# Output biases of two expert mixtures: one bf16 product over 96 rows in place of a small f32 product, on one Trainium2 core

## The chip, the core and the metric

The kernel runs on one core of one Trainium2 chip. A core has a matrix engine (TensorE, here PE), three engines for element-wise work (VectorE or DVE, ScalarE or ACT, GpSimd or POOL), and SyncE (SP), whose queue issues all of this kernel's DMAs. Operands lie in SBUF, matmuls accumulate in PSUM. The metric is the device time of one execution in microseconds (us).

## The reference, cut to what matters

Eight stages work on 625 nodes of 768 features, a graph layer and a mixture of experts in each of four layers. Each stage normalizes its input and adds its result to x. Two of the mixtures have an output bias, and the change is about these:

```python
# layer 1 (cut): 8 experts, two for each node
gates_full = jnp.zeros((T, E)).at[jnp.arange(T)[:, None], top_idx].add(gates)
def body(acc, p):
    w1, bb1, w2, bb2, g = p
    h = jax.nn.gelu(xn2 @ w1 + bb1, approximate=False)
    return (acc + g[:, None] * (h @ w2 + bb2), None)

# layer 2 (cut): 4 experts with 1024 slots each
h = jax.nn.gelu(jnp.einsum('besd,edh->besh', slots, w1) + b1[None, :, None, :])
y = jnp.einsum('besh,ehd->besd', h, w2) + b2[None, :, None, :]
out = jnp.einsum('besd,bnes->bnd', y, combine)
```

In layer 1 the bias' share of a node's output is its 8 gates times the matrix `b2` of 8 x 768. In layer 2 it is the sum of `combine` over each expert's slots (4 numbers for a node) times a matrix of 4 x 768. Layers 0 and 3 have mixtures of the same form as layer 1's, without a bias.

## The kernel before

The nodes are five tiles of 125 (`TILES`). Weights, products and activations are f32. Most large products are done by a scheme of seven half-size products with sums of blocks ahead (on DVE and POOL) and behind (on DVE).

The program is written for a framework that allots each engine its instructions in an order near the written one, and puts in the waits. The trace shows where it departs from the written order: for example the first matmul of product 5 runs ahead of product 7 in `half_rest`.

`experts` (from line 972) is the mixture of layers 0, 1 and 3. Its 1536 hidden columns are 12 chunks of 128, done in pairs. For a pair c, `first(c)` does products 1 and 2, `sums(c)` puts four block sums on POOL (L338 to L342), and `rest(c)` does products 6, 7, 5, 4, 3 (`half_rest`, L412 are its additions) and the gelu (L1010, ACT). A function handed to `half_rest` runs behind product 6. In `rest(0)` that is `choose`: the router's logits are turned (L260) and `gates` works out on DVE which two experts a node takes and with which weights (L935 to L961), then splits each gate into three bf16 parts in the tile `gb`, by five small operations (L964 to L968). In `rest(2)` it is `chosen`: five matmuls with the identity turn `gb` (L1034) and a copy puts it into `gT3`, 24 rows of 625 (L1038). In layer 1 five f32 transposes (L1042) and a copy (L1043) also put the f32 gates into `gT`, 8 rows. `gate(c)` spreads one expert's gate over its 128 hidden rows by a product with a matrix of ones and zeros (L129, 24 rows, bf16) and multiplies the chunk `hg` with it (L1018). `beside` runs some unrelated sums of products (L1309) on DVE, fed by DMAs.

`down` (from line 1059) is the second product, 12 chunks into 2 x 384 columns. Tile 0 is done directly, tiles 1 and 2 and tiles 3 and 4 in pairs, by seven products of six chunks (`prod`, recorded at L136, with additions at L1125). Where there is a bias, tile 0's two products and products 4, 2, 5 and 3 of each pair end with one more f32 matmul of 8 rows, `gT` or `db` times `b2t`. `db` is the difference of the gates of the pair's two tiles (POOL, L1103), since product 3 needs their difference. `b2t` is loaded by one DMA (L978).

`L2_ffn` (from line 1585) ends in a part that works tile by tile. `scale` multiplies the sums of three experts by factors (L1770), `weights` forms the last expert's exponentials (L1725 on DVE, L1728 on ACT), `last_sums` does the last expert's products, its copies, and the factors `fd` of 4 numbers a node (L1837 to L1845). `turn_sums` transposes the tile (L1798), and `fd` with it (L1804). ACT copies the first (L1802, L1805), DVE the second (L1806). `out` does six f32 matmuls (L1817) and one of 4 rows for the bias (L1822), for each half of the columns. The bias is loaded by one DMA (L1787). `final` normalizes the tile for the next stage; it adds the next bias on POOL (L225).

Of the kernel before, what the change touches and what calls it, by code (L numbers as in the profile page):

```python
# [17 lines left out]
N = 625  # L18
# [17 lines left out]
class Net:  # L36
# [362 lines left out]
    def half_rest(self, prods, U2, top, bottom, between=None):  # L399
# [16 lines left out]
        if between:  # L416
            between()
        prod(7, a2)
        add(C21, U2, a2)
        prod(5, b1)  # L420
# [505 lines left out]
    def gates(self, over_all):  # L926
# [35 lines left out]
        gb = sp.tile([P, NT, NEXP, 3], BF16, tag="gb", name="gb", bufs=1)  # L962
        r = sp.tile([P, NT, NEXP], F32, tag="gr", name="gr", bufs=1)
        nc.vector.tensor_copy(gb[:, :, :, 0], lg)  # L964
        nc.vector.tensor_tensor(r, lg, gb[:, :, :, 0], ALU.subtract)
        nc.vector.tensor_copy(gb[:, :, :, 1], r)
        nc.vector.tensor_tensor(r, r, gb[:, :, :, 1], ALU.subtract)
        nc.vector.tensor_copy(gb[:, :, :, 2], r)  # L968
        return gb

    def experts(self, over_all, w1, w2, gelu, b1=None, b2=None, after=None, beside=None):

        nc, tc, a, x = self.nc, self.tc, self.a, self.x
        with tc.tile_pool(name="moe", bufs=1) as big, ExitStack() as up_pool:
            bc = self.column(b1, NF) if b1 else None
            if b2:
                b2t = big.tile([NEXP, D], F32, name="b2t")
                nc.sync.dma_start(b2t, a[b2])  # L978
            hg = big.tile([128, NF, N], F32, name="hg")
            gT3 = big.tile([3 * NEXP, N], BF16, name="gT3")  # L980
            gT = big.tile([NEXP, N], F32, name="gT") if b2 else None
# [20 lines left out]
            def rest(c, between=None):  # L1002
# [11 lines left out]
            def gate(c):  # L1014
                gv = self.nv(self.ps(), 128)
                self.mm_nodes(gv, [sel[:, c * 128 : (c + 1) * 128]], [self.n3(gT3)])
                h = self.n3(hg[:, c, :])
                nc.vector.tensor_tensor(h, h, gv, ALU.mult)  # L1018
# [6 lines left out]
            turned, gb = self.logits(big), []  # L1025

            def choose():
                turned()
                gb.append(self.gates(over_all))

            def chosen():
                pv = self.nv(self.ps(), 3 * NEXP)
                for t in range(NT):
                    nc.tensor.matmul(  # L1034
                        pv[:, t, :], gb[0][:, t].rearrange("p e i -> p (e i)"),
# [3 lines left out]
                if b2:  # L1039
                    pv = self.nv(self.ps(), NEXP)  # L1040
                    for t in range(NT):
                        nc.tensor.transpose(pv[:, t, :], self.lg[:, t, :], self.ident[:P, :P])  # L1042
                    nc.vector.tensor_copy(self.n3(gT), pv)  # L1043

            rest(0, choose)
            for c in range(2, NF + 2, 2):
                if c < NF:
                    if c not in begun:
                        first(c)
                    rest(c, chosen if c == 2 else None)  # L1050
# [1263 lines left out]
```

## Time and profile before

| what | value |
|---|---|
| median of 3 runs | 1917.44 us (1917.02 to 1918.27) |
| the profiled execution | 1917.89 us |
| its span, first to last instruction | 1916.2 us |
| mean granted clock of TensorE | 0.988 |
| busy: PE, DVE, POOL, ACT | 1849.2, 1129.8, 601.8, 526.0 us |
| layer 1's mixture: up products / `down` | from about 717 / 797.2 to 879.7 us |
| layer 2's tile-by-tile part | about 1352 to 1424 us |
| layer 0's and layer 3's gates | about 246 to 257 / 1777 to 1788 us |

The page that the profile prints has the busy time of each engine, the chain of work that ended last, and the costliest groups of instructions. In a group's or timeline's line "L136 PE MATMUL ps<-b2t,gT 8*125 8x384 f32", the first number pair is the stationary operand's rows and columns, the second the moving operand's. In a timeline, the first two numbers are the start and the length in us; lines that belong together are merged, xN tells how many records; the bracket is the engine's idle time before it and what ended it. PEld is the loading of a matmul's stationary operand. A matmul's length includes its way through the array, so the time that one costs in a stream is read from start to start.

### The profile page before, as it was taken

To read this page: it belongs to the slowest core of one execution; us is meant where nothing else is said; L and a number is where in the kernel's file an instruction comes from. 1 tells how busy PE (TensorE), PEld (TensorE's weight loads), DVE (VectorE), ACT (ScalarE), POOL (GpSimd) and SP (SyncE) were. 2 spreads that over 40 slices of the span, in tenths; PEclk is the share of its full clock that TensorE was granted. 3 is DMA by queue.
4 is the path that set the end of the run, shared out by engine and by line. 5 is a ranking of instruction groups with operands and counts; after the bars stand their busy time and mean duration, and the time that the engine had idled before them with its cause. 6 is when DMAs were issued, how large, how long until landed. Compare 5 with 4: busy or idle time off the path is not lost.

```text
span 1916.2 us, 21703 instructions
## 1 busy us (share of the span) xinstructions
PE 1849.2 (97%) x8314; PEld 1273.0 (66%) x8314; DVE 1129.8 (59%) x2227; ACT 526.0 (27%) x960; POOL 601.8 (31%) x514
## 2 busy tenths in 40 slices
PE   7968899999999999999999999999999999999999
PEld 6844565555677766655555788878767888556655
DVE  8789866547566756663935464554545555145552
ACT  2379721002244532100110131331314233111200
POOL 1079634234410052433106322231025321402341
PEclk9969999999999999999999999999999999999999
DMA  2040111211300022213410211001011121020111
GB/s 69 21 143 34 40 53 50 77 58 34 95 13 25 1 99 94 67 53 131 142 66 34 74 64 36 25 25 34 1 44 37 44 66 64 1 99 25 50 33 32
DMA packets 64021, 103.16 MB, mean 54 GB/s; under 512 B 7301, under 2 KB 37223, under 8 KB 63918
## 3 DMA queue, kind: packets, MB, share of 16 engines
q1 hardware_dynamic: 63658, 101.69, 16.1%
q8 instruction: 66, 1.08, 0.2%
q14 instruction: 37, 0.30, 0.1%
q10 hardware_dynamic: 260, 0.09, 0.0%
HBM read 99.81 MB, written 1.95 MB: 53 GB/s over the span
## 4 chain that ended last, share of the span: by engine, by line
PE 86%; DVE 7%; POOL 3%; ACT 2%; issue 1%; DMA 1%; ACTq 0%; DVEq 0%; POOLq 0%; SPq 0%
PE ps L136 66%; PE ps L129 4%; PE ps L777 3%; POOL gat_w L560 2%; PE ps L1817 2%; PE ps L1472 2%; PE ps L1504 2%; PE ps L1491 1%; PE ps L198 1%; PE ps L1686 1%; PE ps L143 1%; PE ps L715 1%; DVE gat_w L591 1%; ACT xT L205 0%; PE ps L2002 0%
## 5 line engine op out<-in xcount | busy, mean ns | idle before, releaser
L338 POOL TENSOR_TENSOR S<-w 128x384 f32<-128x384 f32 x40 | 41.5, 1041 | 445.0 <-PE ps L136 342.6
L136 PE MATMUL ps<-xT,w 128*128 128x313 f32 x480 | 137.4, 429 | 0.7 <-ACT pr L1480 0.7
L136 PE MATMUL ps<-w,xT 128*125 128x384 f32 (+2 forms) x392 | 125.3, 473 | 0.0
L136 PE MATMUL ps<-T,w 128*128 128x313 f32 x408 | 121.5, 428 | 0.0
L560 POOL TENSOR_TENSOR gat_w<-gat_w,xT 125x625 f32<-125x625 f32 x60 | 86.3, 1470 | 100.7 <-DVE xT L532 93.8
L136 PEld LDWEIGHTS ps<-xT,w 128*128 128x128 f32 x480 | 89.0, 190 | 34.6 <-issue 1.8
L136 PE MATMUL ps<-T,S 128*128 128x313 f32 x348 | 104.1, 433 | 1.7 <-DVE T L318 1.4
L136 PEld LDWEIGHTS ps<-w,xT 128*125 128x125 f32 x392 | 72.8, 188 | 46.6 <-issue 11.7
L136 PE MATMUL ps<-xT,S 128*128 128x313 f32 x336 | 101.6, 432 | 0.1
L136 PE MATMUL ps<-w,S 128*125 128x384 f32 x292 | 99.9, 488 | 1.4 <-DVE x L1125 1.4
L136 PE MATMUL ps<-w,hg 128*125 128x384 f32 x288 | 96.5, 488 | 0.9 <-DVE hg L1018 0.9
L136 PEld LDWEIGHTS ps<-T,w 128*128 128x128 f32 x408 | 75.9, 189 | 29.8 <-DVE U L358 1.4
L136 PE MATMUL ps<-hh,gat_w 125*125 125x257 f32 (+1 forms) x400 | 89.8, 379 | 0.0
L136 PE MATMUL ps<-w,x2T 128*125 128x384 f32 (+1 forms) x280 | 84.2, 449 | 0.0
L136 PEld LDWEIGHTS ps<-T,S 128*128 128x128 f32 x348 | 63.7, 189 | 29.4 <-ACT lt L366 4.4
L136 PEld LDWEIGHTS ps<-w,S 128*125 128x125 f32 x292 | 54.4, 188 | 42.2 <-issue 2.2
L136 PEld LDWEIGHTS ps<-hh,gat_w 125*125 125x125 f32 x400 | 73.3, 187 | 11.3 <-issue 0.4
L136 PEld LDWEIGHTS ps<-w,hg 128*125 128x125 f32 x288 | 53.1, 188 | 39.9 <-issue 2.2
L777 PE MATMUL ps<-ohd,ohs 125*125 125x313 bf16 x425 | 66.2, 311 | 12.2 <-DVE ohs L770 12.2
L136 PEld LDWEIGHTS ps<-xT,S 128*128 128x128 f32 x336 | 61.3, 189 | 25.0 <-issue 3.6
L569 DVE CUSTOM_DVE_ANT_0 junk<-ps,mb 125x625 f32<-125x625 f32 x85 | 68.5, 806 | 13.5 <-PE ps L143 8.7
L129 PE MATMUL ps<-gat_w,ft 125*65 125x500 f32 (+1 forms) x240 | 70.5, 450 | 4.5 <-DVE gat_w L591 3.0
(443 smaller groups left out, 3790.2 us busy)
## 6 DMA issues: line engine op xcount, KB each, us to landing
w<-in_L_ffn_phiT SPq DMA_DIRECT2D x8, 1536.0 KB
w<-in_L_gnn_W SPq DMA_DIRECT2D x8, 1536.0 KB
w<-in_L_ffn_w SPq DMA_DIRECT2D x6, 1152.0 KB
w<-in_L_gnn_W SPq DMA_DIRECT2D x6, 1152.0 KB
av_w<-in_L_gnn_W SPq DMA_DIRECT2D x24, 256.0 KB
av_w<-in_L_gnn_W SPq DMA_DIRECT2D x16, 384.0 KB
w<-in_L_ffn_w SPq DMA_DIRECT2D x3, 1536.0 KB
w<-in_L_ffn_qkv_wT SPq DMA_DIRECT2D x6, 768.0 KB
```

Source lines behind the costliest of these rows:

```text
L129: self.nc.tensor.matmul(pv[:, s, :], lhs[i], rhs[i][:, s, :], start=i == 0, stop=i == n - 1)
L136: self.nc.tensor.matmul(out, lhs[i], rhs[i], start=i == 0, stop=i == n - 1)
L143: self.nc.tensor.transpose(pv[:, t, :], col(t).to_broadcast([P, rows]), self.ident[:P, :P])
L198: nc.tensor.transpose(pv[:, k, :P], src[:, k * 128 : (k + 1) * 128], self.ident[:P, :P])
L338: nc.gpsimd.tensor_tensor(S1, A21, A22, ALU.add)
L560: nc.gpsimd.tensor_tensor(w[:, s, :], w[:, s, :], lc[:, s, :], ALU.add)
L569: nc.vector.tensor_tensor_reduce(self.n3(junk), row, self.n3(mb[:, t, :]), 1.0, -3e38, ALU.subtract, ALU.max, m[:, t : t + 1],)
L591: nc.vector.tensor_tensor(ws, ws, row.unsqueeze(1).to_broadcast(ws.shape), ALU.subtract)
L777: nc.tensor.matmul(acc[j // 2][:, j % 2, :], ohs[:, TILES[j]], ohd[:, 0:HN], start=c == cs[0], stop=c == cs[-1],)
L1472: nc.tensor.matmul(sv[r][:, s, :], qk[half[r], 0, TILES[t]], self.n3(qk[half[r], 1, :])[:, s, :], start=True, stop=True,)
L1504: nc.tensor.matmul(ov[half[r]], v[:, s, h * DH : (h + 1) * DH], pT[r][:, s, :], start=s == 0, stop=s == NT - 1,)
L1817: nc.tensor.matmul(pv[:, j, :], zTs[t][:, k, :], w2[k // 3][:, k % 3, js], start=k == 0, stop=False,)
```

## The change

The product of gates and bias is done by one bf16 matmul over 96 rows. A f32 number is the sum of three bf16 parts. Three copies of 32 rows are stacked, 24 of them used in layer 1 (8 experts x 3 parts of the gate), 12 in layer 2 (4 experts x 3 parts of the factor); copy j of the gates meets part j of the bias. All nine products of parts are thus summed in one matmul.

- `gates` writes its parts straight into the first copy, one operation fewer than before, and copies them to the second and third where there is a bias (layer 1). The tile `gb` moves to the stage's own pool, and POOL clears it.
- `b2t` becomes 96 rows: POOL clears it, nine DMAs load it, row by row of the parts. `bias_parts` splits it on POOL, with the last parts' right half negated in `b2n`; it is written behind the rest of chunks 6 and 7, and begins with a copy of one column of `hg`.
- `chosen` turns 96 columns in place of 24; the f32 transposes and `gT` go. It is run behind product 7 in place of product 6, in all three mixtures.
- `down` uses `gT3` and `b2p`. Product 3 gets two bias products, one with the first tile's gates, one with the second tile's and the negated bias; `db` goes.
- `L2_ffn` has the same for its factors: `fp` is split from `fd` in `last_sums` by five more DVE operations, turned by a bf16 matmul written behind ACT's copy, and its bias is loaded by nine DMAs and split on POOL behind the scaling of tile 1.

The diff, cut to its core:

```diff
-    def half_rest(self, prods, U2, top, bottom, between=None):
+    def half_rest(self, prods, U2, top, bottom, between=(None, None)):
...
         prod(6, a1)
         add(U2, U2, a1)
-        if between:
-            between()
+        if between[0]:
+            between[0]()
         prod(7, a2)
         add(C21, U2, a2)
+        if between[1]:
+            between[1]()
         prod(5, b1)
...
-    def gates(self, over_all):
+    def gates(self, over_all, gb):
...
-        gb = sp.tile([P, NT, NEXP, 3], BF16, tag="gb", name="gb", bufs=1)
         r = sp.tile([P, NT, NEXP], F32, tag="gr", name="gr", bufs=1)
-        nc.vector.tensor_copy(gb[:, :, :, 0], lg)
-        nc.vector.tensor_tensor(r, lg, gb[:, :, :, 0], ALU.subtract)
-        nc.vector.tensor_copy(gb[:, :, :, 1], r)
-        nc.vector.tensor_tensor(r, r, gb[:, :, :, 1], ALU.subtract)
-        nc.vector.tensor_copy(gb[:, :, :, 2], r)
-        return gb
+        parts = gb[:, :, 0, 0 : 3 * NEXP].rearrange("p t (e i) -> p t e i", i=3)
+        nc.vector.tensor_copy(parts[:, :, :, 0], lg)
+        nc.vector.tensor_tensor(r, lg, parts[:, :, :, 0], ALU.subtract)
+        nc.vector.tensor_copy(parts[:, :, :, 1], r)
+        nc.vector.tensor_tensor(parts[:, :, :, 2], r, parts[:, :, :, 1], ALU.subtract)
+        for j in range(1, gb.shape[2]):
+            nc.vector.tensor_copy(gb[:, :, j, 0 : 3 * NEXP], gb[:, :, 0, 0 : 3 * NEXP])
...
+            copies, rows = (3, 32) if b2 else (1, 3 * NEXP)
             if b2:
-                b2t = big.tile([NEXP, D], F32, name="b2t")
-                nc.sync.dma_start(b2t, a[b2])
+                b2t = big.tile([96, D], F32, name="b2t")
+                b2p = big.tile([96, D], BF16, name="b2p")
+                b2n = big.tile([96, D // 2], BF16, name="b2n")
+                nc.gpsimd.memset(b2t, 0.0)
+                for j in range(3):
+                    for i in range(3):
+                        r = 32 * j + i
+                        nc.sync.dma_start(b2t[r : r + 3 * NEXP - 2 : 3, :], a[b2])
...
+            gb = big.tile([P, NT, copies, rows], BF16, name="gb")
+            if b2:
+                nc.gpsimd.memset(gb, 0.0)
...
+            def bias_parts(after):
+                nc.gpsimd.tensor_copy(b2p[:, 0:1], after)
+                nc.gpsimd.tensor_copy(b2p, b2t)
+                nc.gpsimd.tensor_tensor(b2t, b2t, b2p, ALU.subtract)
+                for j in range(1, 3):
+                    nc.gpsimd.tensor_copy(b2p[32 * j : 32 * j + 32, :], b2t[32 * j : 32 * j + 32, :])
+                nc.gpsimd.tensor_tensor(b2p[64:96, :], b2t[64:96, :], b2p[64:96, :], ALU.subtract)
+                nc.gpsimd.tensor_scalar(b2n, b2p[:, D // 2 :], -1.0, None, ALU.mult)
...
             def chosen():
-                pv = self.nv(self.ps(), 3 * NEXP)
+                pv = self.nv(self.ps(), copies * rows)
                 for t in range(NT):
                     nc.tensor.matmul(
-                        pv[:, t, :], gb[0][:, t].rearrange("p e i -> p (e i)"),
+                        pv[:, t, :], gb[:, t].rearrange("p j r -> p (j r)"),
                         self.identb[:P, :P], start=True, stop=True,
                     )
                 nc.vector.tensor_copy(self.n3(gT3), pv)
-                if b2:
-                    pv = self.nv(self.ps(), NEXP)
-                    for t in range(NT):
-                        nc.tensor.transpose(pv[:, t, :], self.lg[:, t, :], self.ident[:P, :P])
-                    nc.vector.tensor_copy(self.n3(gT), pv)
-
-            rest(0, choose)
+
+            rest(0, choose, None)
...
-                    rest(c, chosen if c == 2 else None)
+                    rest(c, None, chosen if c == 2 else None)
+                    if b2 and c == 6:
+                        bias_parts(hg[:96, 5, 0:1])
...
-            if b2t is not None:
+            if bias:
                 lhs.append(gT[:, TILES[0]])
-                rhs.append(b2t[:, j * HD : (j + 1) * HD])
+                rhs.append(bias[0][:, j * HD : (j + 1) * HD])
...
-            prod(4, b2, (t + 1, 0))
+            prod(4, b2, (t + 1, bl))
...
-            prod(2, a1, (t, 0))
+            prod(2, a1, (t, bl))
...
-            prod(5, a2, (t + 1, 1))
+            prod(5, a2, (t + 1, br))
...
-            prod(3, b1, (None, 1))
+
+            prod(3, b1, (t, br), (t + 1, bn))
...
+            fp = big.tile([P, NT, 3, 32], BF16, name="fp")
+            nc.gpsimd.memset(fp, 0.0)
...
-                    b2.append(self.rows.tile([NE, D], F32, tag="row", name="b2"))
-                    nc.sync.dma_start(b2[0], a["L2_ffn_b2"])
+                    b = self.rows.tile([96, D], F32, tag="row", name="b2")
+                    nc.gpsimd.memset(b, 0.0)
+                    for j in range(3):
+                        for i in range(3):
+                            r = 32 * j + i
+                            nc.sync.dma_start(b[r : r + 3 * NE - 2 : 3, :], a["L2_ffn_b2"])
+                    b2.append(b)
+
+                def bias_parts(after):
+                    b = b2.pop()
+                    bp = mp.tile([96, D], BF16, tag="M", name="bp")
+                    nc.gpsimd.tensor_copy(bp[:, 0:1], after)
+                    nc.gpsimd.tensor_copy(bp, b)
+                    nc.gpsimd.tensor_tensor(b, b, bp, ALU.subtract)
+                    for j in range(1, 3):
+                        rows = slice(32 * j, 32 * j + 32)
+                        nc.gpsimd.tensor_copy(bp[rows, :], b[rows, :])
+                    nc.gpsimd.tensor_tensor(bp[64:96, :], b[64:96, :], bp[64:96, :], ALU.subtract)
+                    b2.append(bp)
...
-                    nc.tensor.transpose(pv[:NE, n, :], fd[:, t, :], self.ident[:P, :P])
                     nc.scalar.copy(zTs[t][:, ks[0] : ks[-1] + 1, :], pv[:, 0:n, :])
-                    nc.vector.tensor_copy(fTs[t], pv[:NE, n, :])
+                    nc.tensor.matmul(
+                        pv[:96, n, :], fp[:, t].rearrange("p j r -> p (j r)"),
+                        self.identb[:P, :P], start=True, stop=True,
+                    )
+                    nc.vector.tensor_copy(fTs[t], pv[:96, n, :])
...
+                    r = big.tile([P, NE], F32, tag="fr", name="fr", bufs=2)
+                    parts = fp[:, t, 0, 0 : 3 * NE].rearrange("p (e i) -> p e i", i=3)
+                    nc.vector.tensor_copy(parts[:, :, 0], fd[:, t, :])
+                    nc.vector.tensor_tensor(r, fd[:, t, :], parts[:, :, 0], ALU.subtract)
+                    nc.vector.tensor_copy(parts[:, :, 1], r)
+                    nc.vector.tensor_tensor(parts[:, :, 2], r, parts[:, :, 1], ALU.subtract)
+                    nc.vector.tensor_copy(
+                        fp[:, t, 1:3, 0 : 3 * NE],
+                        fp[:, t, 0:1, 0 : 3 * NE].to_broadcast([P, 2, 3 * NE]),
+                    )
...
                 scale(1)
+                bias_parts(Z[:96, 1, 0, 0:1])
                 turn_sums(1, first)
```

## The prediction

> **What bounds the kernel now.** I read the page's first part (busy time), then its chain of waits, then the list of what TensorE waited for, and then the timeline around every line that the diff touches.
>
> ```profile
> PE 1849.2 (97%) x8314; PEld 1273.0 (66%) x8314; DVE 1129.8 (59%) x2227; ACT 526.0 (27%) x960; POOL 601.8 (31%) x514
> ...
> PE 86%; DVE 7%; POOL 3%; ACT 2%; issue 1%; DMA 1%; ACTq 0%; DVEq 0%; POOLq 0%; SPq 0%
> ```
>
> TensorE (PE) is busy 97% and carries 86% of the chain, so a matmul taken out of a stretch without PE idle time is time taken off the end. The list of waits says where PE is idle; only this row of it belongs to the change, three waits of 1.0 us for the gates:
>
> ```profile
> PE ps L1034 <- DVE gb L968: 3.1, 3, 1.0
> ```
>
> The timeline of layer 1's output product shows what a bias product costs:
>
> ```profile
> 797.20 8.01 PE L136 MATMUL ps<-w,hg 128*125 128x384 f32 x24 [0.29 <-DVE hg L1018]
> ...
> 805.14 0.91 PE L136 MATMUL ps<-b2t,gT 8*125 8x384 f32 x2
> ...
> 805.97 8.01 PE L136 MATMUL ps<-w,hg 128*125 128x384 f32 x24
> ```
>
> An f32 matmul is two records here. 24 full records take 805.14 - 797.20 = 7.94, or 0.33 each. The two records of the 8-row bias product hold PE from 805.14 to 805.97: 0.83, more than 2 x 0.33. Layer 2's are alike (4 rows, L1822, 1372.86 to 1373.69: 0.83). There is no PE idle time from 797.2 to 879.7, and about 1.4 us in 59.2 from 1365.0 to 1424.2.
>
> The gates' end in layer 1 (layers 0 and 3 look the same):
>
> ```profile
> 740.09 1.75 PE L136 MATMUL ps<-T,S 128*128 128x313 f32 x6
> ...
> 740.92 0.92 DVE L967 TENSOR_TENSOR gr<-gr,gb 125x40 f32<-125x40 f32 x1
> 741.75 0.99 POOL L342 TENSOR_TENSOR S<-w,S 128x384 f32<-128x384 f32 x1
> 741.88 0.92 DVE L968 CAST gb<-gr 125x40 bf16<-125x40 f32 x1
> ...
> 742.85 0.45 PE L1034 MATMUL ps<-identb,gb 125*24 125x125 bf16 x5 [1.01 <-DVE gb L968]
> ...
> 743.23 0.70 PE L1042 MATMUL ps<-ident,lg 125*8 125x125 f32 x5
> ```
>
> Each of the small DVE operations ends just behind a POOL operation (L968 at 742.80, L342 at 742.74), so each has waited for one. PE has finished product 6 and idles until the gates are split.
>
> **The change, part by part.** The sum is made against the profiled execution, 1917.89 us (span 1916.2); the median of the runs shown is 1917.44, 0.45 lower.
>
> *Bias products.* Removed: 10 in layer 1 (2 for tile 0, 4 for each pair of tiles) and 10 in layer 2 (2 for each tile), 20 x 0.83 = 16.6. Added: 12 in layer 1 (the third half product now takes two) and 10 in layer 2, each one bf16 record of 96 rows and 384 columns. The trace has no 96-row matmul. Nearest rows: the bf16 gate products (L129, 24 rows). One of 500 columns holds PE from 792.17 to 792.49, 0.32; three of 125, 500 and 125 columns from 771.43 to 771.86, 0.43. So 250 columns cost 0.11, or 0.44 ns a column: 384 are 0.17, and 0.10 goes to the run as such. Low end 0.17; high end one record of the 8-row product, 0.83 / 2 = 0.415. The extra appears beside few-row operands (the weight load idles 0.55 around the 8-row product, 0.43 before the 24-row one), not beside 125 rows: the transpose L1804 between 128-row f32 products takes 0.11 (1387.96 to 1388.07). 96 is nearer to 125, so I take 0.20. 22 x 0.20 = 4.4; gain 12.2.
>
> The Trainium skill's page "TensorEngine Tiling (Array Packing)", Key Properties, says that a switch of the array's tiling mode drains the engine, and by its Tiling Modes only up to 64 rows make row tiles. By it 96 rows have no drain: 22 x 0.17, a time 0.7 lower than mine. The 0.55 rows agree with the rule; no row shows 96.
>
> *Turns.* Layer 1's five f32 turns of the gates (L1042) go: 743.23 to 743.76, 0.53. The five bf16 turns load 96 columns for 24: weight loads of 0.093 at 24 columns, 0.137 at 125 (L777), so 0 to 0.2 in all; I take 0.1. Gain 0.4. The f32 copy L1043 (0.79 of DVE) goes too, beside other work: nothing.
>
> *Gates one product later.* PE would reach the turns one product later, 6 x 0.264 = 1.58 (0.264 from 36 records in 9.5 from 717.72): at 742.85 - 1.01 + 1.58 = 743.4 in layer 1. Layers 0 and 3 lose one of the four operations that waited for POOL (L968's 0.92), so the parts are ready at 254.9 against PE at 256.4. Layer 1 gets two copies: the first waits for L342 as L968 did (742.8), the second costs 0.2 (a free cast, L964), ready at 743.0. All three waits go: 3.1. Late next would be the copy of the turned gates, but the first gate product is at 750.2. Ends: 0 and 3.1. The products of DVE's queue behind (C21 of product 4, at 742.70) move 0.3 at most; PE has other PSUM tiles.
>
> *Layer 1's bias split on POOL.* Price: a subtraction of 768 columns 1.81 (L225 undisturbed); a cast lies between the memset rate (0.519 for 512, so 0.78) and 1.81, I take the middle, 1.3. One column, cast, subtraction, two casts, subtraction, half a cast: 0.1 + 2 x 1.81 + 3 x 1.3 + 0.65 = 8.3. Written behind the sums of chunk 8 (end 762.4), so done at 770.7; POOL is idle until 771.59. If this cover is gone, the next sums (end 776.5) are wanted by PE at 787.3. Nothing.
>
> *Queues.* Nine bias loads for one on SP: 0.30 each, +2.4, behind a memset of 0.8 on POOL. They delay the load at 718.38 (used at 801) and the vector rows at 724 (used at 752). On POOL the memset goes ahead of L1536 at 719.59, whose result is read at 815. Layer 2's bias was loaded at 893.17; SP's next entry is at 906.4, and POOL's sums from 893.77 are wanted at 906.2, ended 898.2. The memsets of the gate parts are 0.4 each. Nothing. `db` goes (0.76 of POOL before 3.1 idle): nothing.
>
> *Layer 2's bias split on POOL* starts after the second scaling (1353.0): 0.1 + 3.6 + 3.9 = 7.6. DVE then has three scalings (0.69) and the four subtractions L1725 (5.57), 7.6 together, all with two SBUF operands, which the rows above show taking turns with POOL. Strict turns: the last L1725 ends at 1353.0 + 7.6 + 7.6 - 1.8 = 1366.4, its exponential (1.25) at 1367.7. PE wants that pair at 1365.0 + 12 x 0.169 = 1367.0. Loss 0.7; with casts of 0.78 none, of 1.81 2.2. The parts themselves are wanted at 1372.9, ready about 1368.2.
>
> *Layer 2's factors.* Five small DVE operations a tile, 0.2 each. Only tile 1 feels them: L1806 (1380.07) would move to 1381.07, 0.5 past PE's bias product at 1380.84. Tiles 0, 2 and 3 have 1.4 to 4.6 to spare. Loss 0.5, low end 0.
>
> *The factors' turn behind the ACT copy.* In the trace ACT's copy starts 0.04 after L1804's end though it reads other columns of the same PSUM tile: such accesses seem to be kept in order. Then PE waits for the copy's end in tiles 2, 3, 4: 0.45 + 0.45 + 0.3 = 1.2; nothing if the next products are put ahead. I take 0.6.
>
> **Sum:** -12.2 - 0.4 - 3.1 + 0.7 + 0.5 + 0.6 = -13.9, so 1904.0.
>
> **Rivals.**
>
> *A: 96 rows cost like few rows* (0.415): 22 x 0.215 = 4.7 less, 1908.7. For it: every small-row product in the trace pays. Against: 125 rows do not.
>
> *B: the gates' wait only moves.* Layer 1's margin is 0.4; if the turns come elsewhere in PE's order or DVE's queue is later, 3.1 stay: 1907.1. For it: PE's order already departs from the written one (product 5's first matmul ahead of 7). Against: 1.5 of margin in layers 0 and 3.
>
> *C, slower: POOL's casts.* The only copy rows on POOL are
>
> ```profile
> L274 POOL COPY wide<-v 128x48 f32<-128x48 f32 x1 | 1.0, 1013 | 0.0
> ```
>
> 21 ns an element: 16.2 for 768. Then 3 casts in layer 2 and 3.5 in layer 1 outgrow their cover (4.7 up to 1372.9; 0.9 + 10.8 in layer 1): 3 x 14.9 - 4.7 + 3.5 x 14.9 - 11.7 = 80, 1984. It decides from 6.0 a cast, where 6.5 x 4.7 = 13.9 + 16.4. Against: that copy began at 1425.66 beside DVE's L444 (1425.65 to 1426.59) and ended just after it, so it mostly waited.
>
> The Trainium skill's "SBUF — State Buffer", Who interferes with whom, has this as an exclusive lock on a port pair of DVE and GpSimd. By it the turn-taking in layer 2 is strict, as I sum it; the gates' rows agree.
>
> **Numbers.** Mine 0.70, A 0.12, B 0.09, C 0.05; 0.04 for a larger stall in layer 2's tail that leaves the time near 1915. 0.2% (3.8 us) is about what a measurement tells from no change. All but the last two are faster: 0.91; same 0.04; slower 0.05. Low end: 0.17 a product and no losses, 1904.0 - 0.7 - 1.8 = 1901.5, and 1.5 for a shifted order, 1900. High end: A with all the losses at their ends (+2.1), 1911. Predicted: 1904.
>
> **What would show it.** 96-row records spaced 0.17 to 0.2 in L136 and L1822's successor, without the 0.55 ahead; no PE wait for the gates' DVE lines; a wait of PE for L1728's exponentials under 2.2 near 1365; POOL's split ended before 1372. It is wrong if 96-row records hold PE for 0.4, if a POOL cast takes over 2 us, or if the first up-weights wait on SP behind the nine loads.

## The result and the profile after

The changed kernel takes 1903.41 us (median of 4 runs, 1901.49 to 1903.62), the kernel before 1917.23 on the same chip. The ratio is 0.9925, 95% interval 0.9907 to 0.9942: faster by 0.6 to 0.9%. The profiled execution is one of 1903.34 (span 1901.6, clock 0.987), 14.55 below that of before. 1904.0 was predicted.

The page's busy times and the shares of the chain of waits after the change:

```profile
PE 1834.2 (96%) x8291; PEld 1270.9 (67%) x8291; DVE 1137.9 (60%) x2250; ACT 526.1 (28%) x960; POOL 618.5 (33%) x529
...
PE 82%; DVE 8%; POOL 3%; ACT 2%; issue 2%; DMA 1%; SPq 1%; ACTq 0%; DVEq 0%; POOLq 0%
```

TensorE is busy 15.0 us less, DVE 8.1 more, POOL 16.7 more. The span is 14.6 shorter, so TensorE waits 0.4 more than before, although its waits for the gates went. The timeline of layer 1's output product after (start, length, engine and line):

```profile
794.88 8.01 PE L136 MATMUL ps<-w,hg 128*125 128x384 f32 x24 [0.29 <-DVE hg L1032]
802.72 0.33 PE L136 MATMUL ps<-b2p,gT 96*125 96x384 bf16 x1
802.89 7.90 PE L136 MATMUL ps<-w,hg 128*125 128x384 f32 x24
810.63 0.33 PE L136 MATMUL ps<-b2p,gT 96*125 96x384 bf16 x1
```

A bias product holds PE for 802.89 - 802.72 = 0.17, and the 24 records behind it take 810.63 - 802.89 = 7.74, where they took 7.94 between two 8-row products. Without few-row products beside them these records take 0.3225 each (7.74 / 24). So an 8-row f32 product cost 0.83 and another 0.20 in the records beside it: 8.77 from one bias product to the next (805.14 to 813.91), now 7.91.

What TensorE waited for. These are the rows of the list that changed in or behind the changed stages and that the account below uses:

```profile
PE ps L136 <- DVE x L1143: 2.9, 2, 1.5
PE ps L136 <- ACT U L1151: 2.0, 2, 1.2
...
PE ps L136 <- DVE mb L548: 0.8, 1, 0.8
...
PE ps L2058 <- DVE rden L2042: 0.6, 1, 0.6
PE ps L1847 <- ACT zT L1846: 0.5, 1, 0.5
PE ps L1867 <- DVE zT L1851: 0.5, 1, 0.5
...
PE ps L1058 <- DVE gb L971: 0.2, 1, 0.2
```

The columns are us in total, times, and the longest. The gates' row fell from 3.1 to 0.2. L1143 and L1151 are the additions and a copy in `down`; they were 1.4 and 1.2, once each (L1125 and L1133 before), and the second of each is new and lies in layer 1's `down`. L548 and L2058 are new and lie in layer 3's graph layer.

Executions differ by up to 3 us ahead of layer 0's gates, where all these kernels have the same code (last section). So the experiments are read by stage, from the starts of the same TensorE records in each trace. In us: the waits at the turns in layers 0, 1 and 3; layer 1's turns to its first bias product; from there to layer 2's first bias product; layer 2's first to its last; from there to layer 3's turns; and all from TensorE's arrival at layer 0's turns to its last matmul. A gap of about 0.1 that stands ahead of the 24-column turns of layers 0 and 3 even when nothing is late (0.09 to 0.11) counts as 0. What the table leaves out (layer 0's turns to layer 1's, and layer 3's turns to the end) is 485.7 to 486.1 and 124.5 in all of them.

| kernel | wait L0 | wait L1 | to bias 1 | to bias 2 | tail L2 | to turns L3 | wait L3 | all |
|---|---|---|---|---|---|---|---|---|
| before | 1.03 | 1.01 | 62.29 | 567.72 | 49.86 | 363.17 | 1.03 | 1656.60 |
| after | 0 | 0.24 | 61.60 | 562.24 | 42.95 | 364.46 | 0 | 1641.99 |
| before_one_op_fewer | 0 | 0 | 62.29 | 567.73 | 49.86 | 364.17 | 0 | 1654.61 |
| gates_fifth_op | 1.02 | 1.09 | 61.61 | 561.86 | 42.95 | 364.26 | 1.04 | 1644.31 |
| l1only | 0 | 1.09 | 61.61 | 562.82 | 49.86 | 363.29 | 0 | 1649.21 |
| l2only | 1.03 | 1.01 | 62.29 | 567.74 | 42.94 | 364.24 | 1.02 | 1650.73 |
| f32_96_rows | 0 | 1.09 | 61.61 | 566.08 | 47.32 | 363.96 | 0 | 1650.47 |
| row_ladder | 0 | 1.09 | 61.70 | 564.27 | 44.61 | 364.33 | 0 | 1646.47 |
| gates_four_ops | 0 | 0 | 61.60 | 562.32 | 42.94 | 364.55 | 0 | 1641.74 |
| down_waits | 0 | 1.09 | 61.61 | 560.97 | 42.93 | 364.53 | 0 | 1641.61 |
| fp_before_copy | 0 | 1.10 | 61.61 | 562.37 | 42.82 | 364.38 | 0 | 1642.93 |
| pool_casts_twice | 0 | 1.09 | 61.61 | 562.85 | 42.94 | 364.35 | 0 | 1643.39 |
| tuned_all | 0 | 0 | 61.60 | 560.81 | 42.64 | 364.36 | 0 | 1639.63 |

Kernels whose code is the same in a stage agree to 0.3 in most columns, to 1.0 in "to bias 2" (561.86 to 562.85) and to 1.0 in "to turns L3" (before 363.17, before_one_op_fewer 364.17). Layer 1's wait was 0.24 in the changed kernel's profile and 1.09 or 1.10 in all six others with the same gates. So 0.24 was luck of the phase, by which is meant how operations of DVE and POOL happen to fall beside each other: in that profile the two copies L971 took 0.99 together, in `l1only` 1.84. One more kernel, whose turns stand elsewhere, is told of below.

### The profile page after: what moved, and what is told of

It is laid out like the page before. It is cut to its first block, busy times and chain, and to the rows that moved or that the text cites. A ratio compares the mean times of both kernels' runs of the same rounds, so it can differ in the third digit from the quotient of the medians.

```text
span 1901.6 us, 21718 instructions
## 1 busy us (share of the span) xinstructions
PE 1834.2 (96%) x8291; PEld 1270.9 (67%) x8291; DVE 1137.9 (60%) x2250; ACT 526.1 (28%) x960; POOL 618.5 (33%) x529
## 4 chain that ended last, share of the span: by engine, by line
PE 82%; DVE 8%; POOL 3%; ACT 2%; issue 2%; DMA 1%; SPq 1%; ACTq 0%; DVEq 0%; POOLq 0%
PE ps L136 64%; PE ps L129 4%; POOL gat_w L562 2%; PE ps L779 2%; PE ps L1491 2%; PE ps L1523 2%; PE ps L1862 2%; PE ps L1510 1%; PE ps L198 1%; PE ps L1708 1%; PE ps L143 1%; PE ps L717 1%; DVE gat_w L593 1%; DVE Td L447 0%; DVE Td L448 0%
## 5 line engine op out<-in xcount | busy, mean ns | idle before, releaser
L779 PE MATMUL ps<-ohd,ohs 125*125 125x313 bf16 x425 | 66.2, 311 | 12.2 <-DVE ohs L772 12.2
```

Source lines behind the costliest of these rows:

```text
L779: nc.tensor.matmul(acc[j // 2][:, j % 2, :], ohs[:, TILES[j]], ohd[:, 0:HN], start=c == cs[0], stop=c == cs[-1],)
```

## The experiments

### What a bias product costs: type and rows

The bias products in f32 over 96 rows, most of them zero:

```diff
-                self.down(dp, a[w2], hg, gT3, (b2p, b2n) if b2 else None, after, beside)
+                self.down(dp, a[w2], hg, gTf if b2 else gT3, (b2t, b2n) if b2 else None, after, beside)
...
-                        fTs[t] = zT[:96, NK, :].bitcast(BF16)[:, 0:P]
+                        fTs[t] = zT[:96, NK, :]
```

> The changed kernel, but the 22 bias products are f32 products over 96 rows in place of bf16 ones: the gates' (and factors') parts are turned as before and copied to f32, the f32 bias stands against the first 24 (12) rows, the other rows of the bias are zero, the split on POOL falls away. Same sum, by another route. Theory 'rows': few rows cost extra beside full-row products; over 96 rows a f32 product costs what the others cost, 2 records of 0.3225 = 0.65, so 22 x (0.65 - 0.17) = 10.6 more than the changed kernel: about 1914. Theory 'f32': the 8-row product's 0.83 and the 0.2 around it belong to any f32 product that interrupts the stream, whatever its rows: 22 x (1.03 - 0.17) = 19: about 1922. In the trace: the start-to-start step of a bias product is 0.65 by the first, 0.83 to 1.0 by the second.

Measured: 1911.50 us, ratio 0.9972 (0.9960 to 0.9984).

```profile
803.22 0.81 PE L136 MATMUL ps<-b2t,gTf 96*125 96x384 f32 x2
803.87 7.90 PE L136 MATMUL ps<-w,hg 128*125 128x384 f32 x24
811.61 0.81 PE L136 MATMUL ps<-b2t,gTf 96*125 96x384 f32 x2
```

0.65 a product, and 7.74 for the 24 records: "rows" by its step. The tail is 4.37 longer than the changed kernel's, 9 x 0.48 = 4.3. The total rose less than 10.6 because the stretch with `down` grew by 3.84 for 12 x 0.48 = 5.8: its two waits of 0.83 and 1.43 shrank to one of 0.48.

The bf16 products over fewer rows:

```diff
-                                pv[:, j, :], fTs[t], b2[0][:, js], start=False, stop=True
+                                pv[:, j, :], fTs[t][:K], b2[0][:K, js], start=False, stop=True
```

with `K = (12, 16, 32, 33, 48, 64, 65, 80, 88, 96)[2 * t + j]`, and 24 rows in layer 1.

> The changed kernel with the bf16 bias products over fewer rows: the 12 of layer 1 over 24 rows, the 10 of layer 2 over 12, 16, 32, 33, 48, 64, 65, 80, 88 and 96 rows, in this order. It leaves the products of the bias' second and third parts out, wholly in layer 1 and in part in layer 2. Theory 'rows': a product over few rows costs 0.2 to 0.4 more in the stream (an 8-row f32 product took about 1.0 with what is around it, two full records 0.65), with a step somewhere between 32 and 65 rows: 12 x 0.3 + 4 to 6 x 0.3 = 5 to 6, so 1908 to 1909. Theory 'pass': only the type and its one record count, a bf16 product is 0.17 over any number of rows: 1903.4. The ten steps of layer 2, read in the trace, give the price by rows.

Measured: 1906.62 us, ratio 0.9947 (0.9931 to 0.9964). The steps of layer 2's tiles 2 and 3:

```profile
1384.79 0.49 PE L1862 MATMUL ps<-w,zT 128*125 128x384 f32 x1
1385.21 0.37 PE L1868 MATMUL ps<-bp,zT 48*125 48x384 bf16 x1
1385.51 1.55 PE L1862 MATMUL ps<-w,zT 128*125 128x384 f32 x4
1387.00 0.37 PE L1868 MATMUL ps<-bp,zT 64*125 64x384 bf16 x1
1387.30 0.86 PE L198 MATMUL ps<-ident,xn 125*128 125x125 f32 x6
...
1397.84 0.33 PE L1868 MATMUL ps<-bp,zT 65*125 65x384 bf16 x1
1398.00 1.45 PE L1862 MATMUL ps<-w,zT 128*125 128x384 f32 x4
1399.29 0.33 PE L1868 MATMUL ps<-bp,zT 80*125 80x384 bf16 x1
```

From one bias product to the next, with four f32 records between: 1.79 at 48 rows, 1.45 at 65. At 12 and at 32 rows it is 1.79 and 1.78, at 88 rows 1.45. So up to 64 rows a product costs 0.34 more: 0.14 in its own step (0.30 for 0.16) and 0.20 in the full records between two of them (1.49 for 1.29). The record right ahead of the 48-row product takes 0.42 for 0.32, and the rest falls on the one right behind a few-row product. By the own step the change lies between 64 rows (0.30) and 65 (0.16). With the f32 kernel the four prices are: f32 over 4 or 8 rows 1.03, f32 over 96 rows 0.65, bf16 over 12 to 64 rows 0.50, bf16 over 65 to 96 rows 0.16 to 0.17. Of the 0.86 that each old product gave up, 0.33 to 0.38 are rows and 0.48 to 0.53 the type. The total stayed below 1908. In layer 1 the extra shows as 2.0, because `down`'s waits fell from 2.26 to 1.01, and because two few-row products in a row (product 3 has two) pay the extra once: 0.33 for the pair. Eight single ones and two pairs are 3.4, less 1.25 of waits 2.1.

### The gates: an operation, not a place

In the changed kernel's trace the turns (L1058) still stand right behind product 6, as before. Layer 0:

```profile
252.84 1.04 DVE L968 CAST gb<-gr 125x40 bf16<-125x40 f32 x1
253.06 1.75 PE L136 MATMUL ps<-T,S 128*128 128x313 f32 x6
253.78 0.99 POOL L341 TENSOR_TENSOR w<-w 128x384 f32<-128x384 f32 x1
253.91 0.94 DVE L969 TENSOR_TENSOR gb<-gr,gb 125x40 bf16<-125x40 f32 x1
254.73 1.00 POOL L342 TENSOR_TENSOR S<-w,S 128x384 f32<-128x384 f32 x1
254.90 0.45 PE L1058 MATMUL ps<-identb,gb 125*24 125x125 bf16 x5
```

So the later written place did not move the turns on TensorE, and what is left of the edit is the operation fewer. To test it, the fifth operation is put back:

```diff
-        nc.vector.tensor_tensor(parts[:, :, :, 2], r, parts[:, :, :, 1], ALU.subtract)
+        nc.vector.tensor_tensor(r, r, parts[:, :, :, 1], ALU.subtract); nc.vector.tensor_copy(parts[:, :, :, 2], r)
```

> The changed kernel with one edit undone: the gates' third part is again made by two DVE operations (a subtraction into r and a cast), five for four, in all three mixtures. The written place of the turns (behind product 7) stays. Theory 'operation': the waits of TensorE for the gates went because one DVE operation that waits for a POOL operation fell away, since the changed trace still shows the turns right behind product 6. Then the wait comes back by 0.9 to 1.0 in layer 0 and in layer 3, and layer 1's 0.24 grows by 0.2 to 0.9: 1905.4 to 1906.2 us against 1903.4. Theory 'place' (my prediction's step: TensorE reaches the turns one product, 1.58 us, later): layers 0 and 3 have 1.5 of margin, the operation costs at most 0.4 in layer 1: 1903.4 to 1903.8, with no wait at the turns in layers 0 and 3.

Measured: 1904.80 us, ratio 0.9934 (0.9919 to 0.9949), span 2.2 longer. The waits are back in layers 0 and 3 (1.02 and 1.04). Layer 1's 1.09 shows nothing, since six kernels without the fifth operation have it too. The reverse, in the kernel before:

```diff
-        nc.vector.tensor_tensor(r, r, gb[:, :, :, 1], ALU.subtract)
-        nc.vector.tensor_copy(gb[:, :, :, 2], r)
+        nc.vector.tensor_tensor(gb[:, :, :, 2], r, gb[:, :, :, 1], ALU.subtract)
```

> The kernel before with one edit: the gates' third part is written by the subtraction itself, so that one DVE cast falls away in each of the three mixtures. Bias products, turns and their written place stay. Theory 'operation': the three waits of 1.0 at the turns (1.03 in layers 0 and 3, 1.01 in layer 1) fall to about 0.1, because the operation that goes had waited 0.9 for a POOL operation: -2.8, about 1914.2 on the chip where the kernel before takes 1917.0. Theory 'place': it is the later place that takes the waits away, so that without it at least layer 1's wait stays: 1916 to 1917.

Measured: 1913.98 us for 1916.89, ratio 0.9983 (0.9973 to 0.9992). All three waits are gone, 3.07 in all; 1.0 of it comes back in layer 3's graph layer, by a phase (last section). And the later place, made real while the fifth operation is there:

```diff
-        if between[1]:
-            between[1]()
         prod(5, b1)
+        if between[1]:
+            between[1]()
```

> The changed kernel with the fifth DVE operation of the gates back, as in the run where that alone brought all three waits back (1.02, 1.09 and 1.04 us), and with the turns written behind product 5 in place of product 7. Written behind product 7 they still came out right behind product 6 on TensorE; written behind product 5 they come out behind product 7 and half of product 5, six matmul records (1.58 us) later. If a later place is worth what my prediction gave it, it hides the operation: no wait at the turns in any of the three layers, 3.1 less than the run with the fifth operation alone, 1901.7 to 1902.5. Rival: the copy of the turned gates, or the additions behind it on DVE, then hold up product 4 or the first gate products: 1903.5 to 1904.8, with new waits for L1062 or L412.

Measured: 1905.35 us, ratio 0.9937 (0.9921 to 0.9954): no faster than with the fifth operation alone. The expectation's six records were wrong: the turns came out twelve records (3.16 us) later, behind the whole of products 7 and 5. There they wait no longer. TensorE waits elsewhere, in layer 0 so:

```profile
252.22 0.92 DVE L969 CAST gb<-gr 125x40 bf16<-125x40 f32 x1
253.04 0.47 DVE L412 TENSOR_TENSOR hg<-hg,ps 128x313 f32<-128x313 f32 x1
253.44 0.47 DVE L412 TENSOR_TENSOR U<-U,ps 128x313 f32<-128x313 f32 x1
...
254.05 1.82 PE L136 MATMUL ps<-T,w 128*128 128x313 f32 x6 [0.83 <-DVE U L412]
```

The addition to U reads product 6 from one half of a PSUM tile, and product 7 writes the other half (`a1` and `a2` in `half_rest`). In this trace product 7 begins behind that addition in all 18 places, 0.14 us behind it here, and the addition stands behind the gates in DVE's queue. 0.83, 0.82 and 0.84 took the place of 1.02, 1.09 and 1.04. The rival was right about the wait; the time came out above its range.

In layer 1 the two copies L971 make the gates late again. Writing all copies by the splitting operations:

```diff
-        nc.vector.tensor_copy(parts[:, :, :, 0], lg)
+        nc.vector.tensor_copy(parts[:, :, :, :, 0], every(lg))
```

(`parts` over all copies, `every` a read repeated for each, the two other operations alike, L971 gone.)

> The changed kernel, with the gates' parts written into all three copies by the splitting operations themselves (repeated reads), so that layer 1's two copies L971 go. In the changed kernel's profile layer 1 waited 0.24 at the turns; three other kernels with the same gates waited 1.09, because the first copy stood behind POOL's last block sum. Theory 'operation': with four operations layer 1 is like layers 0 and 3: no wait, so 0.2 to 1.1 less, 1902.3 to 1903.2. Rival: the wider operations (120 columns for 40) take longer beside POOL and the wait stays: 1903.4.

Measured: 1901.87 us, ratio 0.9924 (0.9909 to 0.9939). No wait in any layer. Layer 1's 0.24 is gone by stage, and against the 1.09 of the six others the edit is worth 1.1. The ratio alone does not tell it from the changed kernel's 0.9925.

### Where the gain was given back

> The kernel before with the change in the three mixtures alone (gates, turns, layer 1's bias products and split); layer 2's tail is the old one. My prediction's steps for this part: -5.9 (10 x 0.83 less 12 x 0.2) - 0.4 - 3.1 = -9.4: 1908.0. From the shifts between the two traces: layer 0's gates -0.96, layer 1 up to its output product -1.36, the output product -5.64, layer 3's gates -0.93 = -8.9: 1908.5. A rival: the 1.9 that the changed kernel gives back in layer 3's graph layer comes from this part too (its order of DVE work): about 1910.

The kernel before with the diff's parts for `half_rest`, `gates`, `experts` and `down`. Measured: 1910.78 us, ratio 0.9965 (0.9952 to 0.9978); by stage 7.4 less than before, for 8.9 expected. Missing are 0.85 at layer 1's turns and 0.6 in `down`. Layer 3's graph layer takes 363.29, as before: the rival falls.

> The kernel before with layer 2's part of the change alone (factors, their turn, the ten bias products, the split). My prediction's steps: 10 x (0.83 - 0.2) = -6.3, and 0.7 + 0.5 + 0.6 lost: -4.5, about 1912.5 where the kernel before takes 1917.0. From the shifts between the two traces: the tail from the last exponentials to layer 3's projection is 7.6 shorter, and 1.2 to 1.9 come back in layer 3's graph layer, where DVE's block sums stand in another order and TensorE waits for its mask copies and its reciprocal: -5.7 to -6.4, 1910.6 to 1911.3. The kernel with the three mixtures alone has no such waits in layer 3's graph layer, so they should appear here. If they don't, they need both parts, and the time is 1909.4.

The kernel before with the diff's part for `L2_ffn`. Measured: 1911.77 us, ratio 0.9973 (0.9962 to 0.9984); by stage 5.9 less. The tail is 6.92 shorter, and its two waits in layer 3's graph layer appear:

```profile
PE ps L136 <- DVE mb L546: 0.8, 1, 0.8
...
PE ps L2039 <- DVE rden L2023: 0.5, 1, 0.5
```

The first of them belongs to layer 2's part of the change: neither the kernel before nor the one with the mixtures alone has it. The second doesn't (last section).

In `down` the changed kernel's wait of 1.43 looks so:

```profile
829.44 0.55 DVE L1143 TENSOR_TENSOR x<-x,ps 125x384 f32<-125x384 f32 x1
831.10 0.69 DVE L1328 CUSTOM_DVE_ANT_0 av_junk<-av_w,av_a 128x512 f32<-128x512 f32 x1 [1.11 <-DMA av_w<-in_L_gnn_W]
...
833.15 0.69 DVE L1328 CUSTOM_DVE_ANT_0 av_junk<-av_w,av_a 128x512 f32<-128x512 f32 x1 [0.62 <-DMA av_w<-in_L_gnn_W]
...
834.50 0.55 DVE L1143 TENSOR_TENSOR x<-x,ps 125x384 f32<-125x384 f32 x1
...
835.10 1.23 PE L136 MATMUL ps<-w,S 128*125 128x384 f32 x3 [1.43 <-DVE x L1143]
```

What TensorE wants to begin at 835.10 is product 5, not product 3 as the expectation below has it: twelve records (the line ends with the window shown, at 836) and then one bias product follow, while product 3 has two. The addition at 834.50 reads product 2 from the other half of product 5's PSUM tile, and ahead of it in DVE's queue stand sums that wait for transfers. Before, TensorE's longer products hid this; the two kernels with dearer bias products agree, with waits of 1.01 (`row_ladder`) and 0.48 (`f32_96_rows`) here.

```diff
-            add(x21, b2)
+            add(x21, b2); bias and beside(1, x21[:, 0:1])
...
-                beside(7, U3[:, 0:1])
+                beside(*((1, x12[:, 0:1]) if bias else (7, U3[:, 0:1])))
```

(The same behind the additions of products 2 and 5.)

> The changed kernel, with layer 1's sums of attention products (L1328, seven pairs in one go behind product 7's addition) dealt out one pair at a time behind the additions of products 4, 2, 5 and 3 of both pairs of tiles. In the changed kernel DVE waited 1.11 and 0.62 for the transfers that feed them, with the addition that frees a PSUM bank queued behind, and TensorE waited 1.43 at product 3. Theory 'DVE's queue': that wait goes: 1902.0. Rival: TensorE's wait only moves to the second pair of tiles, where the sums now stand too: 1903.4, with waits for L1143 near 860.

Measured: 1901.69 us, ratio 0.9921 (0.9907 to 0.9936). The stretch to layer 2's first bias product is 1.27 shorter than the changed kernel's. Its list keeps the 0.83, and the 0.3 ahead of `down` that the kernel before has too:

```profile
PE ps L136 <- ACT U L1151: 0.8, 1, 0.8
PE ps L136 <- DVE hg L1032: 0.3, 1, 0.3
```

### Layer 2's tail

```diff
-                    nc.scalar.copy(zTs[t][:, ks[0] : ks[-1] + 1, :], pv[:, 0:n, :])
                     nc.tensor.matmul(
                         pv[:96, n, :], fp[:, t].rearrange("p j r -> p (j r)"),
                         self.identb[:P, :P], start=True, stop=True,
                     )
+                    nc.scalar.copy(zTs[t][:, ks[0] : ks[-1] + 1, :], pv[:, 0:n, :])
```

> The changed kernel with one edit undone in layer 2's tail: the factors' turn is written ahead of ScalarE's copy of the turned tile, as in the kernel before. In the changed kernel TensorE waited 0.47 for that copy and then 0.47 for the turned factors of tile 1, whose DVE copy L1851 stood behind seven small operations. Theory 'place of the turn' (my prediction's step of 0.6, and its 0.5 for tile 1): both waits go, since L1851 comes out some operations earlier in DVE's order: -0.9, about 1902.5. Rival: the turn then holds up ScalarE's copy, and TensorE waits for that at the next products instead: 1903.4, or more.

Measured: 1903.74 us, ratio 0.9927 (0.9910 to 0.9943); the tail is 0.13 shorter. The waits only change places:

```profile
1369.73 1.55 PE L1862 MATMUL ps<-w,zT 128*125 128x384 f32 x4 [0.46 <-ACT zT L1850]
1371.72 0.38 PE L1867 MATMUL ps<-bp,zT 96*125 96x384 bf16 x1 [0.44 <-DVE zT L1851]
```

The product behind the turn needs ACT's copy too, and the kernel before had the same wait there:

```profile
1379.36 1.55 PE L1817 MATMUL ps<-w,zT 128*125 128x384 f32 x4 [0.46 <-ACT zT L1805]
```

```diff
-                    nc.gpsimd.tensor_copy(bp, b)
+                    nc.gpsimd.tensor_copy(bp, b); nc.gpsimd.tensor_copy(bp, b); nc.gpsimd.tensor_copy(bp, b)
```

> The changed kernel with two more full casts of layer 2's bias on POOL behind the second scaling (1.25 to 1.9 us each), nothing else. My prediction had DVE and POOL take strict turns there, so that the last exponentials come late and TensorE waits 0.7; the profile showed no wait and 0.4 to spare. Theory 'strict turns': POOL's 2.5 to 3.8 more push DVE's four subtractions back by as much, and TensorE waits 2.1 to 3.4 at the last sums: 1905.5 to 1906.8. Theory 'partial': DVE lost 4.1 of POOL's 10.8 us before, so it loses some 40% of the extra, 1.0 to 1.5, and TensorE waits 0.6 to 1.1: 1904.0 to 1904.5.

Measured: 1903.83 us, ratio 0.9926 (0.9911 to 0.9941), the tail as long as the changed kernel's. Neither theory held. The changed kernel, and then this one:

```profile
1347.24 2.03 POOL L1823 TENSOR_TENSOR b<-b,bp 96x768 f32<-96x768 f32 x1
...
1347.70 9.70 DVE L1747 TENSOR_TENSOR lt<-lt,mrow 128x1250 f32<-128x1250 f32 x4
...
1353.35 2.73 POOL L1827 TENSOR_TENSOR bp<-b,bp 32x768 bf16<-32x768 f32 x1
```

```profile
1346.29 4.54 POOL L1822 CAST bp<-b 96x768 bf16<-96x768 f32 x3
...
1348.08 8.88 DVE L1747 TENSOR_TENSOR lt<-lt,mrow 128x1250 f32<-128x1250 f32 x4
...
1357.73 1.63 POOL L1827 TENSOR_TENSOR bp<-b,bp 32x768 bf16<-32x768 f32 x1
```

DVE's four subtractions lose 4.1 and 3.3 against the 5.57 they take alone. With 3.3 more of casts ahead, POOL's last subtraction comes after DVE's last in place of beside it (1.63 for 2.73). So DVE's loss did not grow with POOL's work; that each of its operations loses at most one turn would explain it, and was not tested further.

### All edits together

The three edits that helped or might (`gates_four_ops`, `down_waits`, `fp_before_copy`), and the factors' parts written into all copies at once:

```diff
-                    nc.vector.tensor_copy(parts[:, :, 0], fd[:, t, :])
+                    nc.vector.tensor_copy(parts[:, :, :, 0], every(fd[:, t, :]))
```

> The changed kernel with four edits together: the gates' and layer 2's factors' parts written into all copies by the four splitting operations, layer 1's sums of attention products dealt out behind the additions, and the factors' turn ahead of ScalarE's copy. If the waits are independent of each other, the gains add: 1.5 (down) + 0.24 to 1.09 (gates) + 0.9 (turn): 1899.9 to 1900.8. If one only uncovers the next, as the changed kernel's shorter stretches did: 1901.5 to 1902.

Measured: 1901.13 us (1898.40 to 1901.26), ratio 0.9909 (0.9894 to 0.9923). By stage it is 2.4 below the changed kernel's profile and 3.2 below what that is with the usual wait of 1.09 in layer 1; the intervals of the two ratios overlap, so it is the stages that say it is faster. Of that, `down` has 1.4, the gates 0.2 to 1.1 and the tail 0.3, so the first two add as expected. The tail gave 0.3 of the expected 0.9, and the total fell between the two ranges.

## Why the prediction came out right

1904.0 was right to 0.6 us, and inside the range. The direction and the main cause, cheaper bias products, were right, but the closeness is luck: the bias products gave 4.7 more than forecast and the tail lost 1.2 less, while 4.9 of waits and delays were not in the sum at all, and the gates' waits went by another way than forecast.

| step | predicted | shown |
|---|---|---|
| bias products | -12.2 | -16.9 |
| f32 turns of layer 1 | -0.4 | -0.7 |
| gates' waits | -3.1 | -2.8 |
| bias split in layer 1, queues | 0 | 0 |
| layer 2's bias split | +0.7 | 0 |
| factors' operations | +0.5 | +0.5 |
| factors' turn behind the copy | +0.6 | +0.1 |
| waits in `down` | none | +2.3, and 0.5 in small pieces |
| layer 3's graph layer | none | +2.1 |

The sum of the right column is -14.9 for a measured -14.6.

*Bias products.* The mis-sized term. I charged an 8-row product its two records, 0.83, and left out what it does to its neighbours, though the trace of before showed 0.33 a record beside it, where full records among themselves take 0.3225: 20 x 1.03 - 22 x 0.17 = 16.9. The low end, 0.17, was the price of 96 rows. Rival A (0.415 for 96 rows) is false, and the ladder puts the step between 64 and 65 rows.

*Turns.* I let 96 columns cost 0.1 more than 24. They cost 0.14 less: the last of layer 0's five 24-column turns and the record behind it take 0.148 and 0.368 (255.13 to 255.65), those of layer 1's 96-column turns 0.055 and 0.320. With the 0.53 of the f32 turns that is the 0.7 shown. So few columns of the stationary operand cost a bf16 product something too; where that step lies no run shows.

*Gates.* The step "PE would reach the turns one product later" failed: the order did not change, and where it does change (fifth_op_later_turns) a wait of 0.83 takes the place of 1.0. I had judged that DVE's queue behind moves "0.3 at most; PE has other PSUM tiles", and that is what failed: product 7 goes into the tile that product 6 is still read from. In layers 0 and 3 the waits went by the operation fewer, which the step named for these two. In layer 1 the two copies take it back: the margin of 0.4 was not there, and its wait was 0.24 in the profile but 1.1 in six other kernels, so 0.8 of the 2.8 is luck of this profile. Rival B, that the wait only moves, is what the later place does, and what layer 1 does in those six; its time was not seen, because in layers 0 and 3 the operation that goes was enough.

*Bias splits.* POOL's full cast took 1.31 in layer 1 and 1.25 in layer 2 (1.3 taken), so rival C with 16.2 a cast is false. Layer 1's split took 8.5 (760.0 to 768.5) for 8.3. In layer 2 I charged DVE 5.8; it lost 4.1, and the last exponentials ended at 1358.7, 0.4 before PE wanted them.

*Queues.* A load of the bias held SP for 0.62 to 0.75, not 0.30, nine for 6.1 in layer 1. It hid all the same.

*Factors.* Tile 1's wait of 0.47 is the predicted one; in `tuned_all`, with an operation fewer for the factors, it is 0.25 for the 0.44 of `fp_before_copy`. The turn behind the copy costs 0.1, because the next product waits for the copy anyway.

*Not in the sum.* "No PE idle time" in `down` meant that DVE and ACT kept just ahead of TensorE; with bias products 0.86 shorter, 0.83 (ACT's copy L1151, behind a square root that waits for DVE) and 1.43 came to light. `down_waits` shows the cause of the 1.43; no run takes away the 0.83 alone, but it is gone in both kernels with dearer bias products. In the other kernels with the changed `down` as it is the 1.43 is 1.20 to 1.80. The stretch up to layer 3's turns grew by 1.3 although the bias product that it begins with is 0.86 shorter. That makes the 2.1. 1.2 of them lie ahead of record L287, where DVE does its block sums (L446 to L449) in another order, and the mask copies L548 come late behind them; that the order is the cause was not tested by itself. 0.9 is the phase below.

## What to carry to other kernels

Price a small matmul in a stream by the whole step from its predecessor's start to its successor's, with its neighbours' slowing: here 0.34 us of a bf16 product and 0.38 of an f32 product went with few rows (up to 64 measured in bf16, 4 and 8 in f32). Where TensorE is never idle, its suppliers may stand just behind it: a shorter product turns their queues into waits, so look for what stands ahead of the operation that reads the other half of its PSUM tile. Moving a consumer later in one queue hides a late producer only if nothing else in the producer's queue is wanted sooner.

## What the runs showed of the chip that I had not expected

*The step at 64 rows* is sharp: a bf16 product's own step is 0.30 at 64 rows and 0.16 at 65. The Trainium skill's "TensorEngine Tiling (Array Packing)", Key Properties, says that a change of tiling mode drains the engine, and under Tiling Modes gives row tiles of 32 and 64 rows. The ladder agrees, on products that nobody had asked to tile, and gives the price, 0.34 us for going into few rows and out again. Two few-row products in a row pay 0.33 together, which fits a switch; that it is one is inferred from these times.

*Who comes first decides.* In layer 3's graph layer the same DVE operation took 0.43 when it began 50 ns ahead of a POOL sum, and 1.80 when it began 290 ns behind one; the next reciprocal and TensorE (0.63) were late by it. Before, and then after:

```profile
1492.01 0.43 DVE L1994 TENSOR_SCALAR zm<-z 125x512 f32<-125x512 f32 x1
1492.06 2.04 POOL L445 TENSOR_TENSOR Tw<-Tw,w 128x768 f32<-128x768 f32 x1
```

```profile
1477.28 1.81 POOL L447 TENSOR_TENSOR Tw<-Tw,w 128x768 f32<-128x768 f32 x1
1477.57 1.80 DVE L2050 TENSOR_SCALAR zm<-z 125x512 f32<-125x512 f32 x1
```

The kernel before with one gates' operation fewer has unchanged work there, but lost the same 0.9 (its L1994 took 1.89): a phase, not the change. The Trainium skill's "SBUF — State Buffer", Who interferes with whom, says of DVE instructions in its 2-port modes, which it lets `tensor_scalar` enter, that whoever issues first gets the ports shared with GpSimd for the whole instruction and the other fully blocks. These rows agree: the late one ended 0.28 behind the POOL sum.

*The clock.* Executions differ by up to 3.1 us before layer 0's gates. The slice of 25 us from 100 of the changed kernel, and then of row_ladder, whose gates came 2.8 earlier; the granted clock is the third number from the right:

```profile
100.00:125.00 25.00, 14.30 (x48) 10.24 (x47) 20.84 (x34) 20.59 (x35) 22.04 (x21) 0.50 0.75 250
```

```profile
100.00:125.00 25.00, 14.09 (x45) 9.27 (x45) 20.83 (x35) 20.46 (x35) 22.83 (x22) 0.60 0.76 256
```

In the next slice it is 0.84 and 0.93. The code of this stretch is the same in both. The other traces fit: in that next slice six more executions with gates at 254.5 to 255.1 have 0.84 or 0.85, five at 253.3 to 253.8 have 0.86, and fifth_op_later_turns, whose product 6 came 2.6 earlier than the changed kernel's, has 0.93. That the clock is what moves the gates is read from this and was not tested.
